# Attention's input, results and statistics in chunks of 384 columns, a loop bound over all tables, and new timetables

## The chip, the cores and the metric

The kernel runs on one core of a Trainium2 chip. The metric is device time in microseconds, the median of several runs. Before the change it is 9664.73 us (three runs, 9664.22 to 9666.31).

## What is computed

Eight images of 256 channels and 48 x 48 = 2304 positions pass two layers, each with a residual: x + layer(groupnorm(x)). Layer 0 is attention over the 16 nearest positions, layer 1 two Mamba blocks (a selective scan) along the positions.

```python
# layer 0
feat_pos = tokens @ W.T + bias            # feat: 256 columns, pos: 256 columns
pos = pos / jnp.maximum(norm, 1e-12)
sim = jnp.einsum('bnc,bmc->bnm', pos, pos)
topksim, topkid = jax.lax.top_k(sim, K)   # K = 16
attn = jax.nn.softmax(topksim, axis=-1)
out = jnp.einsum('bnk,bnkc->bnc', attn, topkfeat)
# layer 1, twice: layernorm, in_proj, convolution of 4 taps, silu, x_proj, softplus, then over t
h = h * jnp.exp(dt_t[:, :, None] * A) + dt_t[:, :, None] * B_t[:, None, :] * x_t[:, :, None]
y = jnp.einsum('bds,bs->bd', h, C_t)      # 512 channels, 16 states each
# then y = (y + xc * D) * silu(z), and out_proj
...
x = x + _L0_conv_ref(_gn(x), ...)
x = x + _L1_conv_ref(_gn(x), ...)
```

## The kernel before

**Units, steps and parts.** The scan is cut in units: one image, one chunk of T = 384 positions (NCH = 6 chunks an image), one of two depths d, so 12 units an image and 96 in all. Their order in an image is (c,d) = 00, 10, 20, 01, 30, 11, 40, 21, 50, 31, 41, 51. A unit has 16 steps of 32 channels (their 16 states lie on the partitions and in four column blocks), and a step has two parts, so a unit has 32 parts and an image 384. The main loop (L1069) runs over parts m, and one part is one scan of two state blocks on DVE (`run_scan`, L886).

**What a part does.** In program order: `carry` and `decay` on ACT (L902, L871: exp of dt times A for the next part, into one of two PSUM buffers), at even parts `make_bx` on POOL (L847: B times dt x, two steps ahead, into one of eight buffers) and `pool_part` on POOL (L914), then the entries of the table `inner` for this m, then the scan, then the entries of `outer`, then one step of the attention of the next image (`ahead.go`). The product of the state with C is made either by POOL for the parts of a step that are marked G in SHARE, or by DVE (L888) right behind the scan for the parts marked V. SHARE has three strings of 32 letters: for units beside attention (order 1 to 9 in the image), for the units around it (0, 10, 11), and for the last image, which has no attention beside it.

**The tables.** All other work of a unit is placed by hand at parts relative to the unit's first one, from -42 (`load_v`) to 40 (`leave` 1): `between` holds what is issued before that part's scan, `behind` what is issued after it. Entries whose place in m falls beside attention use these; all others use `between_spare` and `behind_spare` (L1026, `beside_none`). Every entry issues to the engines' in-order queues: `in_proj`, `step_size`, `x_proj`, `sum_states`, `out_proj` to PE, `load_*` to SP's DMA queue, `tap`, `copy_z`, `silu_*`, `softplus`, `square`, `root` to ACT, `taps`, `center`, `scale`, `gate` to DVE, `times_x` to POOL with two stores on SP. `sum_states` (L926, k = 0 to 3) adds the states of four steps on PE; when it has read them their `bx` buffers come free. `gate` (L937) multiplies the sum by silu(z) on DVE. `out_proj` (L945) makes two halves, and `leave` (L955) takes each out of PSUM: on ACT with a store for d = 0 (`vo`, L963), on DVE for d = 1 (L967). PE's results of the units and of attention share one ring of four PSUM banks (`mm`, L606), so a new result waits until the one four before it is read.

**Attention.** `layer0` is a generator; `ahead.go` takes one step of it per part, the first at m = EARLY. It projects six chunks, waits for a fixed place modulo 16 parts, and then runs 18 blocks of 128 rows, one every 16 parts, by the table `within` (part, function, argument): `similar` (PE, L445), `keep_similar` (ACT, L454), `top` (DVE, L466 to L473, four passes over 2304 columns), `others` (ACT), `turn` (PE), `weights` (ACT), `weigh` (PE), `average` (ACT and the load of x, L520 to L527), `turn_back` (PE), `finish` (L537). `average` of a block loads 128 columns of x (128 KB), and `finish` two parts later adds the block's result to it (DVE, L541), takes `bn_stats` of both channel halves (L543) and stores 128 columns of x1. After the 18 blocks `group_stats` aggregates (L189). Chunk loads of x for layer 0 and the residual of layer 1 share three buffers with the tag "x". Image 0 has its attention before the scan loop, with nothing beside it (`alone`).

Of the kernel before, what the change touches and what calls it, by code (L numbers as in the profile page):

```python
# [8 lines left out]
F32 = mybir.dt.float32  # L9
# [6 lines left out]
P = 128  # L16
# [9 lines left out]
def tile_conv_preact(  # L26
# [18 lines left out]
    nc = tc.nc  # L45
# [5 lines left out]
    CB = C // P  # L51
    DB = DI // P
    NB = N // P
    T = 384
    NCH = N // T
    TB = T // P
# [11 lines left out]
    BLOCK = 16  # L68
    TOPK = (1, 10)
    PHASE = 6  # L70
    EARLY = -24


    SHARE = (
        "GGVGGGVVGGGGGGVGGGVVGGGVGGGGGVVG",
        "GVGGVGVVGVVVGVGVGGGGVGVVGVGVGVGV",
        "VGVGVGVGVGVVGGGVGGGVVGVVGVVGGGVG",
    )
    assert N % T == 0 and N % P == 0 and T % P == 0 and NS % (J * HQ) == 0

# [179 lines left out]
    def layer0(b, left, pool, ps0, alone):  # L260
# [3 lines left out]
        more = 2 if alone else 1  # L264
# [149 lines left out]
        yield  # L414

        x1 = hbm.tile([C, N], F32, tag="x1", name=f"x1_{b}")
        st1 = small.tile([P, CB, NB, 6], F32, tag="gn_st1", name=f"st1_{b}", bufs=1)
        widths = [(c0, min(SW, N - c0)) for c0 in range(0, N, SW)]
        PT = 4
        blocks = [{} for _ in range(NB)]  # L420
# [99 lines left out]
        def average(t):  # L520
            row = blocks[t]
            row["o"] = pool.tile([P, C], F32, tag="o", name=f"o_{b}_{t}", bufs=more)
            nc.scalar.activation(row["o"], row["po"], AF.Identity, scale=row["den"])
            row["xr"] = pool.tile([P, CB, P], F32, tag="xr", name=f"xr_{b}_{t}", bufs=more)
            nc.sync.dma_start(
                row["xr"], x[b, :, t * P : (t + 1) * P].rearrange("(k p) t -> p k t", p=P)
            )  # L527

        def turn_back(t):
            row = blocks[t]  # L530
# [5 lines left out]

        def finish(t):  # L537
            row = blocks[t]
            xr = row["xr"]

            nc.vector.tensor_add(xr, xr, row["pr"].rearrange("p (k t) -> p k t", k=CB))  # L541
            for cb in range(CB):
                nc.vector.bn_stats(st1[:, cb, t, :], xr[:, cb, :])  # L543
            nc.sync.dma_start(x1[:, t * P : (t + 1) * P].rearrange("(k p) t -> p k t", p=P), xr)
            row.clear()


        within = [
            (21, weights, 3), (4, top, 3), (14, turn, 0), (15, weights, 0), (7, others, 3), (-5, similar, 4),
            (-8, keep_similar, 0), (-5, keep_similar, 2), (24, turn_back), (18, weigh, 1), (17, weigh, 0),  # L550
            (1, top, 1), (-9, similar, 0), (-8, similar, 1), (-7, similar, 2), (22, average), (-6, similar, 3),
            (-7, keep_similar, 1), (-3, keep_similar, 3), (0, top, 0), (-3, keep_similar, 4), (15, turn, 1),
            (10, others, 4), (5, others, 0), (3, top, 2), (6, add_top), (11, invert), (5, others, 2),
            (17, turn, 2), (20, turn, 3), (15, weights, 1), (18, turn, 4), (18, weights, 2), (21, weigh, 3),
            (7, others, 1), (19, weigh, 2), (20, weights, 4), (21, weigh, 4), (24, finish),
        ]
        begin = min(part for part, *_ in within)
        parts = {}
# [17 lines left out]
    with tc.tile_pool(name="first", bufs=1) as pool0, tc.tile_pool(  # L576
        name="first_ps", bufs=1, space=PSUM
# [229 lines left out]
    def silu_z(unit):  # L807
# [3 lines left out]
        for e in range(DB - 1):  # L811
# [11 lines left out]
             dt=[], dt_d={}, dtx_d={}, dtr={}, dtxr={}, bx={}, y={}, inw={}, dmat={}, taps={}, xi={}, cv={},  # L823
# [131 lines left out]
    def leave(unit, cb):  # L955
# [16 lines left out]


    between = [
        (-35, center), (7, in_proj, 5), (24, sum_states, 2), (-33, variance), (-21, in_proj, 0),
        (-15, taps, 1), (37, out_proj, 0), (-15, taps, 2), (-14, taps, 3), (-34, square), (39, leave, 0),
        (23, load_rep, "dt", 14), (5, load_rep, "dt", 5), (-4, load_bc, 1), (38, out_proj, 1), (17, load_d, 2),
        (-17, tap, 1), (18, load_rep, "dtx", 13), (-8, times_x, 1), (19, gate, 1), (-22, normal),
        (1, load_rep, "dt", 3), (0, load_rep, "dtx", 4), (15, load_rep, "dt", 10), (6, load_rep, "dtx", 7),
        (10, load_rep, "dtx", 9), (11, gate, 0), (-29, spread_root), (0, times_x, 3), (-19, load_in, 5),  # L980
        (33, load_out), (8, load_rep, "dtx", 8), (-22, load_in, 0), (21, load_rep, "dt", 13), (-20, tap, 0),
        (-10, step_size, 1), (9, copy_z, 2), (-18, in_proj, 2), (2, load_rep, "dtx", 5), (10, sum_states, 0),
        (13, load_rep, "dt", 9), (29, gate, 2), (9, silu_z), (7, load_rep, "dt", 6), (19, load_rep, "dt", 12),
        (-6, load_rep, "dtx", 1), (-14, load_in, 7), (-30, root), (9, load_rep, "dt", 7), (4, load_d, 1),
        (-24, load_in, 3), (17, load_rep, "dt", 11), (14, load_rep, "dtx", 11), (-13, x_proj),
        (-17, load_in, 6), (-3, load_d, 0), (4, load_rep, "dtx", 6), (-4, load_rep, "dtx", 2), (-42, load_v),
    ]
    behind = [
        (-12, split), (-3, load_rep, "dt", 1), (3, in_proj, 4), (-10, step_size, 0), (-3, load_rep, "dt", 0),
        (-8, load_rep, "dtx", 0), (-15, tap, 3), (-1, load_rep, "dt", 2), (-28, scale),  # L990
        (16, load_rep, "dtx", 12), (11, load_rep, "dt", 8), (8, in_proj, 6), (17, sum_states, 1),
        (-14, silu_x), (28, load_rep, "dt", 15), (-39, affine), (2, times_x, 2), (7, copy_z, 0),
        (19, load_rep, "dtx", 14), (10, load_rep, "dtx", 10), (-17, tap, 2), (-10, softplus),
        (-16, in_proj, 3), (3, load_rep, "dt", 4), (-29, load_in, 2), (6, in_proj, 7), (35, gate, 3),
        (-2, load_rep, "dtx", 3), (8, copy_z, 1), (40, leave, 1), (22, load_rep, "dtx", 15), (-8, load_in, 4),
        (29, load_d, 3), (-37, mean), (-19, taps, 0), (-19, in_proj, 1), (-10, load_bc, 0),
        (33, sum_states, 3), (-30, root_end), (-9, times_x, 0), (-20, load_in, 1),
    ]
    between_spare = [
        (24, sum_states, 2), (-34, variance), (-21, in_proj, 0), (38, out_proj, 0), (-15, taps, 2),  # L1000
        (-14, taps, 3), (-35, square), (39, leave, 0), (20, load_rep, "dt", 14), (5, load_rep, "dt", 5),
        (-4, load_bc, 1), (38, out_proj, 1), (17, load_d, 2), (-17, tap, 1), (18, load_rep, "dtx", 13),
        (-8, times_x, 1), (19, gate, 1), (-22, normal), (9, load_rep, "dtx", 8), (1, load_rep, "dt", 3),
        (0, load_rep, "dtx", 4), (14, load_rep, "dt", 10), (6, load_rep, "dtx", 7), (10, load_rep, "dtx", 9),
        (-18, taps, 0), (12, load_rep, "dtx", 10), (17, load_rep, "dtx", 14), (11, gate, 0), (-1, times_x, 2),
        (-19, load_in, 5), (33, load_out), (-22, load_in, 0), (21, load_rep, "dt", 13), (-20, tap, 0),
        (-10, step_size, 1), (9, copy_z, 2), (-18, in_proj, 2), (2, load_rep, "dtx", 5), (10, sum_states, 0),
        (13, load_rep, "dt", 9), (29, gate, 2), (9, silu_z), (7, load_rep, "dt", 6), (19, load_rep, "dt", 12),
        (-6, load_rep, "dtx", 1), (-14, load_in, 7), (37, gate, 3), (-31, root), (9, load_rep, "dt", 7),
        (5, load_d, 1), (-24, load_in, 3), (17, load_rep, "dt", 11), (14, load_rep, "dtx", 11), (-13, x_proj),  # L1010
        (-17, load_in, 6), (-3, load_d, 0), (4, load_rep, "dtx", 6), (-4, load_rep, "dtx", 2), (-42, load_v),
        (-36, center), (-26, spread_root),
    ]
    behind_spare = [
        (-12, split), (-3, load_rep, "dt", 1), (4, in_proj, 4), (-10, step_size, 0), (-5, load_rep, "dt", 0),
        (-8, times_x, 3), (-8, load_rep, "dtx", 0), (-15, tap, 3), (-1, load_rep, "dt", 2),
        (16, load_rep, "dtx", 12), (11, load_rep, "dt", 8), (8, in_proj, 6), (17, sum_states, 1),
        (-14, silu_x), (25, load_rep, "dt", 15), (-39, affine), (6, copy_z, 0), (-17, tap, 2), (-10, softplus),
        (-16, in_proj, 3), (7, in_proj, 5), (3, load_rep, "dt", 4), (-27, load_in, 2), (6, in_proj, 7),
        (-15, taps, 1), (-2, load_rep, "dtx", 3), (8, copy_z, 1), (40, leave, 1), (22, load_rep, "dtx", 15),  # L1020
        (-16, load_in, 4), (29, load_d, 3), (-38, mean), (-21, in_proj, 1), (-12, load_bc, 0),
        (33, sum_states, 3), (-31, root_end), (-9, times_x, 0), (-25, load_in, 1), (-25, scale),
    ]
    place = {(f, *args): part for part, f, *args in between + behind}

# [12 lines left out]
    class Ahead:  # L1038
# [16 lines left out]
        def go(self, m):  # L1055
            if self.image == B or m < EARLY:
                return
# [6 lines left out]
            self.started = self.begun is not None and (m + 1 - PHASE - self.begun) % BLOCK == 0  # L1064

    ahead = Ahead()
    first = min(part for part, *_ in between + behind)
    last = max(part for part, *_ in between + behind)
    for m in range(first, PARTS * NSTEP - HOOKS + last + 1):  # L1069
        n, p = divmod(m, PARTS)  # L1070
        carry(m - 1)
# [56 lines left out]
```

## Time and profile before

| what | value |
|---|---|
| median of three runs | 9664.73 us |
| the profiled execution | 9663.76 us, its span 9661.6 us |
| DVE busy | 8951.2 us |
| POOL busy | 8894.5 us |
| PE / ACT busy | 7986.9 / 7303.4 us |
| L847, `make_bx` on POOL, 1536 times | 5302.0 us, 3458 ns each |
| L871, decays on ACT, 6144 times | 3591.6 us, 585 ns each |
| L886, scans on DVE, 3072 times | 5327.3 us, 1746 and 1753 ns |
| L914, POOL's product, whole steps / half steps | 666 of 3188 ns / 657 of 1692 ns |
| L888, DVE's product of one part, 1083 times | 1037.6 us, 958 ns each |
| first scan | 462.6 us |

Busy time is the union of an engine's instructions. A line of the waits says which instruction of an engine stood idle before it began, and whose end released it: total, times, longest. A line of the timeline has start, duration, engine, source line, operation and tiles, and in brackets the idle time before it.

### The profile page before, as it was taken

The numbers are of one execution on the slowest core, as the hardware profiler recorded it, in microseconds if no ns is written. First come the engines' busy times: TensorE is split into PE (matmuls) and PEld (weight loads), VectorE is DVE, ScalarE is ACT, GpSimd is POOL, SyncE is SP. The second block draws the span as 40 slices with busy tenths as digits, with TensorE's granted clock in tenths as the row PEclk, the third lists the DMA queues.
The fourth block names the chain that finished last, engine by engine and source line by source line (L and its number), as shares of the span: only waits on it lengthen the run. The fifth ranks groups of instructions, "written<-read, shape, count | busy, mean of one in ns | idle before, by whom it ended". The sixth has DMA issues, their size and how long they took to land. (4 is left out here: it accounts for less than half of the span.)

```text
span 9661.6 us, 120523 instructions
## 1 busy us (share of the span) xinstructions
PE 7986.9 (83%) x36761; PEld 4482.3 (46%) x36761; DVE 8951.2 (93%) x7812; ACT 7303.4 (76%) x16018; POOL 8894.5 (92%) x3983
## 2 busy tenths in 40 slices
PE   8888887888878887888878888788887888866665
PEld 6645544455444554445544555444544455432222
DVE  5599998999989999999999999999999999999998
ACT  4587877777777777777777787777787778777776
POOL 1199999999999999999999999999999999999999
PEclk9989998899979998899988999889998899977777
DMA  1134444434444444444444444444444443444443
GB/s 35 57 126 133 125 142 146 135 126 133 136 152 128 132 131 150 136 131 131 135 146 138 130 128 137 146 138 127 135 128 159 128 133 125 143 138 137 148 146 119
DMA packets 1084999, 1267.54 MB, mean 131 GB/s; under 512 B 109728, under 2 KB 1057440, under 8 KB 1084352
## 3 DMA queue, kind: packets, MB, share of 16 engines
q1 hardware_dynamic: 1083808, 1259.83, 40.8%
q8 instruction: 294, 4.82, 0.2%
q14 instruction: 353, 2.89, 0.1%
q10 hardware_dynamic: 544, 0.00, 0.0%
HBM read 1046.58 MB, written 212.86 MB: 130 GB/s over the span
## 5 line engine op out<-in xcount | busy, mean ns | idle before, releaser
L847 POOL TENSOR_TENSOR bx<-BC,dtxr 128x1536 f32<-128x1536 f32 x1536 | 5302.0, 3458 | 124.5 <-PE y L932 106.4
L871 ACT ACTIVATE da<-dtr,A_sb 128x385 f32<-128x385 f32 x6144 | 3591.6, 585 | 960.0 <-DVE bx L886 703.8
L886 DVE TENSOR_TENSOR_SCAN bx<-da,bx 128x770 f32<-128x770 f32 x1989 | 3428.3, 1746 | 153.7 <-ACT da L871 116.9
L914 POOL TENSOR_TENSOR bx<-bx,BC 128x1536 f32<-128x1536 f32 (+1 forms) x1323 | 3234.8, 2445 | 107.6 <-DVE bx L886 101.1
L886 DVE TENSOR_TENSOR_SCAN da<-da,bx 128x770 f32<-128x770 f32 x1083 | 1899.0, 1753 | 65.0 <-ACT da L871 42.3
L932 PE MATMUL y<-bx,sel 128*32 128x384 f32 x12288 | 1323.5, 539 | 181.4 <-POOL bx L914 160.9
L516 PE MATMUL po<-feat,aT 128*128 128x256 f32 x5184 | 1377.7, 415 | 58.1 <-ACT dt L784 44.1
L645 PE MATMUL pe<-vn,inw 128*128 128x384 f32 (+1 forms) x3072 | 1206.0, 524 | 243.8 <-ACT vn L722 71.7
L445 PE MATMUL psim<-pos 128*128 128x512 f32 x2520 | 1220.6, 620 | 100.0 <-DVE xc L745 78.8
L516 PEld LDWEIGHTS po<-feat,aT 128*128 128x128 f32 x5184 | 1036.8, 207 | 405.3 <-ACT dt L784 114.1
L888 DVE TENSOR_TENSOR bx<-da,BC 128x768 f32<-128x768 f32 x1083 | 1037.6, 958 | 37.3
L932 PEld LDWEIGHTS y<-bx,sel 128*32 128x32 f32 x12288 | 426.0, 118 | 1048.7 <-issue 700.9
L645 PEld LDWEIGHTS pe<-vn,inw 128*128 128x128 f32 x3072 | 577.1, 200 | 707.6 <-issue 117.0
L445 PEld LDWEIGHTS psim<-pos 128*128 128x128 f32 x2520 | 501.7, 212 | 649.3 <-issue 382.0
L745 DVE SCALAR_TENSOR_TENSOR xc<-pe,cw,xc 128x384 f32<-128x384 f32 x1152 | 696.0, 611 | 35.0 <-ACT xc L737 8.0
L505 ACT ACTIVATE aT<-pt 128x512 f32<-128x512 f32 (+1 forms) x720 | 387.3, 548 | 354.7 <-PE pt L497 353.1
L496 PE MATMUL pt<-ident,sim 128*128 128x128 f32 x2592 | 551.5, 291 | 104.0 <-ACT sim L454 57.3
L692 PE MATMUL lv<-ones_mean,lsq 128*128 128x1 f32 x1152 | 233.4, 330 | 477.1 <-ACT lsq L686 477.1
L902 ACT COPY h_st<-da 128x2 f32<-128x2 f32 x878 | 139.8, 159 | 583.9 <-DVE bx L888 581.4
L950 PE MATMUL pw<-z,ow 128*128 128x384 f32 x1536 | 539.4, 498 | 42.3 <-DVE z L938 42.0
L775 PE MATMUL pd<-dbl,dtp_sb 16*128 16x384 f32 x768 | 418.4, 691 | 148.2 <-ACT dbl L768 121.5
L496 PEld LDWEIGHTS pt<-ident,sim 128*128 128x128 f32 x2592 | 379.3, 146 | 277.9 <-ACT sim L454 71.6
(156 smaller groups left out, 10322.3 us busy)
## 6 DMA issues: line engine op xcount, KB each, us to landing
dtxr<-dtx_d SPq DMA_DIRECT2D x1536, 192.0 KB, 2.9
dtr<-dt_d SPq DMA_DIRECT2D x1536, 192.0 KB, 2.8
BC<-bc_d SPq DMA_DIRECT2D x192, 768.0 KB, 5.7
inw<-in_in_wT_dram SPq DMA_DIRECT2D x768, 128.0 KB, 2.5
dtx_d<-dtx SPq DMA_DIRECT2D x384, 192.0 KB, 1.9
dt_d<-dt SPq DMA_DIRECT2D x384, 192.0 KB, 2.1
ow<-in_out_wT_dram SPq DMA_DIRECT2D x96, 512.0 KB, 4.1
dmat<-diag SPq DMA_DIRECT2D x384, 64.0 KB, 3.2
```

Source lines behind the costliest of these rows:

```text
L445: nc.tensor.matmul(pm, pos[:, k, t * P : (t + 1) * P], pos[:, k, c0 : c0 + w], start=(k == 0), stop=(k == CB - 1),)
L496: nc.tensor.transpose(pt[:, q], row["sim"][:, r], ident)
L516: nc.tensor.matmul(row["po"], aT[:, m % PT, :], feat[:, m, :], start=(m == 0), stop=(m == NB - 1))
L645: nc.tensor.matmul(pe, w[:, k], unit["vn"][:, k, lo:], start=(k == 0), stop=(k == CB - 1))
L745: nc.vector.scalar_tensor_tensor(unit["xc"][e], unit["pe"][e][:, k : k + T], cw[:, unit["d"], e, k : k + 1], unit["xc"][e], ALU.mult, ALU.add,
L847: nc.gpsimd.tensor_tensor(bx[:, :, 1:], unit["BC"][0], unit["dtxr"][i].unsqueeze(1).to_broadcast([P, Q, T]), ALU.mult,)
L871: nc.scalar.activation(da[:, s * (1 + T) : (s + 1) * (1 + T)], unit["dtr"][i], AF.Exp, scale=A_sb[:, unit["d"], i, p * HQ + s : p * HQ + s ...
L886: nc.vector.tensor_tensor_scan(h, da, g, 0.0, ALU.mult, ALU.add)
L888: nc.vector.tensor_tensor(bx[:, :, 0:T], da.rearrange("p (q t) -> p q t", q=HQ)[:, :, 1:], unit["BC"][1][:, qs], ALU.mult,)
L914: nc.gpsimd.tensor_tensor(g[:, :, 0:T], g[:, :, 1:], unit["BC"][1][:, qs], ALU.mult)
L932: nc.tensor.matmul(y[j * G : (j + 1) * G, :], sel, unit["bx"][k * J + j][:, q, 0:T], start=False, stop=True, skip_group_check=True,)
L950: nc.tensor.matmul(pw, unit["ow"][:, k, cb * P : (cb + 1) * P], unit["z"][k], start=(k == 0), stop=(k == DB - 1),)
```

## The change

Four edits, in code:

```diff
-    EARLY = -24
+    EARLY = -22
...
-        "GGVGGGVVGGGGGGVGGGVVGGGVGGGGGVVG",
-        "GVGGVGVVGVVVGVGVGGGGVGVVGVGVGVGV",
-        "VGVGVGVGVGVVGGGVGGGVVGVVGVVGGGVG",
+        "GGVGGGVGGGVVGGVGGGGVGGGVGGGGGVVG",
+        "GVGGGGVVGGVVGGGVVGGGVGVVGVGVGVGV",
+        "VVVGVVGGVGVVGGGVGGGVGGVVGVVGGGVG",
...
-        st1 = small.tile([P, CB, NB, 6], F32, tag="gn_st1", name=f"st1_{b}", bufs=1)
+        rows = {}
+        st1 = small.tile([P, CB, NCH, 6], F32, tag="gn_st1", name=f"st1_{b}", bufs=1)
...
             nc.scalar.activation(row["o"], row["po"], AF.Identity, scale=row["den"])
-            row["xr"] = pool.tile([P, CB, P], F32, tag="xr", name=f"xr_{b}_{t}", bufs=more)
-            nc.sync.dma_start(
-                row["xr"], x[b, :, t * P : (t + 1) * P].rearrange("(k p) t -> p k t", p=P)
-            )
+            if t % TB == 0:
+                tag, bufs = ("xr", 2) if alone else ("x", 3)
+                rows[t // TB] = load_chunk(pool, x[b], t // TB, tag, f"xr_{b}_{t}", bufs)
...
-            xr = row["xr"]
-
+            c, j = divmod(t, TB)
+            xr = rows[c][:, :, j * P : (j + 1) * P]
             nc.vector.tensor_add(xr, xr, row["pr"].rearrange("p (k t) -> p k t", k=CB))
-            for cb in range(CB):
-                nc.vector.bn_stats(st1[:, cb, t, :], xr[:, cb, :])
-            nc.sync.dma_start(x1[:, t * P : (t + 1) * P].rearrange("(k p) t -> p k t", p=P), xr)
+            if j + 1 == TB:
+                xr = rows.pop(c)
+                for cb in range(CB):
+                    nc.vector.bn_stats(st1[:, cb, c, :], xr[:, cb, :])
+                nc.sync.dma_start(x1[:, c * T : (c + 1) * T].rearrange("(k p) t -> p k t", p=P), xr)
...
-    first = min(part for part, *_ in between + behind)
-    last = max(part for part, *_ in between + behind)
+    every = between + behind + between_spare + behind_spare
+    first = min(part for part, *_ in every)
+    last = max(part for part, *_ in every)
```

The rows of x, of the sum and of its statistics are thus kept by chunks of three blocks: one load of 384 KB at the first block's `average`, one store and two `bn_stats` of 384 columns at the third block's `finish`. The loop's bounds are taken over the spare tables too. In the tables these entries change their part (b: `between`, before the scan; h: `behind`, after it); all others keep theirs:

| table | entry: from -> to |
|---|---|
| within | top 0: 0 -> -1; invert: 11 -> 12; weigh 0: 17 -> 16; weigh 2: 19 -> 20; weights 4: 20 -> 19 |
| between, behind | square: -34 b -> -35 h; load_in 1: -20 h -> -21 b; load_rep dt 0: -3 h -> -3 b; times_x 3: 0 b -> -3 b; load_d 1: 4 b -> 5 h; in_proj 7: 6 h -> 5 h; copy_z 1: 8 h -> 8 b; gate 1: 19 b -> 21 b; sum_states 2: 24 b -> 25 b; gate 2: 29 b -> 29 h; sum_states 3: 33 h -> 32 b; leave 1: 40 h -> 38 h |
| spare tables | center: -36 b -> -37 h; spread_root: -26 b -> -29 b; scale: -25 h -> -28 h; taps 3: -14 b -> -14 h; load_rep dt 0: -5 h -> -5 b; load_rep dt 2: -1 h -> -1 b; load_rep dtx 9: 10 b -> 11 b; load_rep dt 14: 20 b -> 23 b; sum_states 2: 24 b -> 25 b; gate 2: 29 b -> 31 b; load_d 3: 29 h -> 29 b |

More of the change, by code (lines that the diff above doesn't have):

```diff
@@ L538, in finish @@
             row = blocks[t]
-            xr = row["xr"]
+            c, j = divmod(t, TB)
+            xr = rows[c][:, :, j * P : (j + 1) * P]
             nc.vector.tensor_add(xr, xr, row["pr"].rearrange("p (k t) -> p k t", k=CB))
-            for cb in range(CB):
-                nc.vector.bn_stats(st1[:, cb, t, :], xr[:, cb, :])
-            nc.sync.dma_start(x1[:, t * P : (t + 1) * P].rearrange("(k p) t -> p k t", p=P), xr)
+            if j + 1 == TB:
[3 more added lines that the diff above has]
+                nc.sync.dma_start(x1[:, c * T : (c + 1) * T].rearrange("(k p) t -> p k t", p=P), xr)
             row.clear()
         within = [
[L549 to L555, printed above, removed]
+            (21, weights, 3), (20, weigh, 2), (4, top, 3), (14, turn, 0), (15, weights, 0), (7, others, 3),
+            (-5, similar, 4), (-8, keep_similar, 0), (-5, keep_similar, 2), (24, turn_back), (18, weigh, 1),
+            (16, weigh, 0), (1, top, 1), (-9, similar, 0), (-8, similar, 1), (-7, similar, 2), (22, average),
+            (-6, similar, 3), (-7, keep_similar, 1), (-3, keep_similar, 3), (-1, top, 0),
+            (-3, keep_similar, 4), (15, turn, 1), (10, others, 4), (5, others, 0), (3, top, 2), (6, add_top),
+            (12, invert), (5, others, 2), (17, turn, 2), (20, turn, 3), (24, finish), (15, weights, 1),
+            (18, turn, 4), (18, weights, 2), (21, weigh, 3), (7, others, 1), (19, weights, 4), (21, weigh, 4),
         ]
@@ L974, in tile_conv_preact @@
     between = [
-        (-35, center), (7, in_proj, 5), (24, sum_states, 2), (-33, variance), (-21, in_proj, 0),
-        (-15, taps, 1), (37, out_proj, 0), (-15, taps, 2), (-14, taps, 3), (-34, square), (39, leave, 0),
+        (-35, center), (7, in_proj, 5), (25, sum_states, 2), (-33, variance), (-21, in_proj, 0),
+        (-15, taps, 1), (37, out_proj, 0), (-15, taps, 2), (-14, taps, 3), (32, sum_states, 3), (39, leave, 0),
         (23, load_rep, "dt", 14), (5, load_rep, "dt", 5), (-4, load_bc, 1), (38, out_proj, 1), (17, load_d, 2),
-        (-17, tap, 1), (18, load_rep, "dtx", 13), (-8, times_x, 1), (19, gate, 1), (-22, normal),
+        (-17, tap, 1), (18, load_rep, "dtx", 13), (-8, times_x, 1), (21, gate, 1), (-22, normal),
@@ L979, in tile_conv_preact @@
         (1, load_rep, "dt", 3), (0, load_rep, "dtx", 4), (15, load_rep, "dt", 10), (6, load_rep, "dtx", 7),
[L980 to L983, printed above, removed]
@@ L984, in tile_conv_preact @@
-        (-6, load_rep, "dtx", 1), (-14, load_in, 7), (-30, root), (9, load_rep, "dt", 7), (4, load_d, 1),
+        (10, load_rep, "dtx", 9), (11, gate, 0), (-29, spread_root), (-20, tap, 0), (-3, times_x, 3),
+        (-19, load_in, 5), (33, load_out), (-3, load_rep, "dt", 0), (8, load_rep, "dtx", 8), (-22, load_in, 0),
+        (21, load_rep, "dt", 13), (-10, step_size, 1), (9, copy_z, 2), (-18, in_proj, 2),
+        (2, load_rep, "dtx", 5), (-21, load_in, 1), (10, sum_states, 0), (13, load_rep, "dt", 9), (9, silu_z),
@@ new lines, in tile_conv_preact @@
+        (7, load_rep, "dt", 6), (19, load_rep, "dt", 12), (-6, load_rep, "dtx", 1), (-14, load_in, 7),
+        (-30, root), (9, load_rep, "dt", 7), (-24, load_in, 3), (17, load_rep, "dt", 11),
+        (14, load_rep, "dtx", 11), (-13, x_proj), (8, copy_z, 1), (-17, load_in, 6), (-3, load_d, 0),
+        (4, load_rep, "dtx", 6), (-4, load_rep, "dtx", 2), (-42, load_v),
+    ]
+    behind = [
+        (-12, split), (3, in_proj, 4), (-10, step_size, 0), (-8, load_rep, "dtx", 0), (-15, tap, 3),
+        (-1, load_rep, "dt", 2), (-28, scale), (16, load_rep, "dtx", 12), (-35, square),
+        (11, load_rep, "dt", 8), (8, in_proj, 6), (17, sum_states, 1), (-14, silu_x), (28, load_rep, "dt", 15),
+        (-39, affine), (2, times_x, 2), (7, copy_z, 0), (19, load_rep, "dtx", 14), (10, load_rep, "dtx", 10),
+        (-17, tap, 2), (-10, softplus), (-16, in_proj, 3), (35, gate, 3), (3, load_rep, "dt", 4),
+        (-3, load_rep, "dt", 1), (-29, load_in, 2), (5, in_proj, 7), (-2, load_rep, "dtx", 3), (38, leave, 1),
+        (22, load_rep, "dtx", 15), (-8, load_in, 4), (29, load_d, 3), (-37, mean), (-19, taps, 0),
+        (5, load_d, 1), (-19, in_proj, 1), (-10, load_bc, 0), (-30, root_end), (-9, times_x, 0), (29, gate, 2),
+    ]
@@ new lines, in tile_conv_preact @@
+    between_spare = [
+        (25, sum_states, 2), (-34, variance), (-21, in_proj, 0), (38, out_proj, 0), (-15, taps, 2),
+        (-35, square), (39, leave, 0), (23, load_rep, "dt", 14), (5, load_rep, "dt", 5),
+        (-1, load_rep, "dt", 2), (-4, load_bc, 1), (38, out_proj, 1), (17, load_d, 2), (-17, tap, 1),
+        (18, load_rep, "dtx", 13), (-8, times_x, 1), (19, gate, 1), (-22, normal), (9, load_rep, "dtx", 8),
+        (1, load_rep, "dt", 3), (0, load_rep, "dtx", 4), (14, load_rep, "dt", 10), (6, load_rep, "dtx", 7),
+        (11, load_rep, "dtx", 9), (-18, taps, 0), (12, load_rep, "dtx", 10), (17, load_rep, "dtx", 14),
+        (11, gate, 0), (-1, times_x, 2), (-19, load_in, 5), (33, load_out), (-22, load_in, 0), (29, load_d, 3),
+        (21, load_rep, "dt", 13), (-20, tap, 0), (-10, step_size, 1), (-5, load_rep, "dt", 0), (9, copy_z, 2),
+        (-18, in_proj, 2), (2, load_rep, "dtx", 5), (10, sum_states, 0), (13, load_rep, "dt", 9),
+        (31, gate, 2), (9, silu_z), (7, load_rep, "dt", 6), (19, load_rep, "dt", 12), (-6, load_rep, "dtx", 1),
+        (-14, load_in, 7), (37, gate, 3), (-31, root), (9, load_rep, "dt", 7), (5, load_d, 1),
@@ L985, in tile_conv_preact @@
         (-24, load_in, 3), (17, load_rep, "dt", 11), (14, load_rep, "dtx", 11), (-13, x_proj),
         (-17, load_in, 6), (-3, load_d, 0), (4, load_rep, "dtx", 6), (-4, load_rep, "dtx", 2), (-42, load_v),
[L987 to L1012, printed above, removed]
@@ L1013, in tile_conv_preact @@
+        (-29, spread_root),
     ]
     behind_spare = [
-        (-12, split), (-3, load_rep, "dt", 1), (4, in_proj, 4), (-10, step_size, 0), (-5, load_rep, "dt", 0),
-        (-8, times_x, 3), (-8, load_rep, "dtx", 0), (-15, tap, 3), (-1, load_rep, "dt", 2),
+        (40, leave, 1), (-12, split), (-14, taps, 3), (-3, load_rep, "dt", 1), (4, in_proj, 4),
+        (-10, step_size, 0), (-8, times_x, 3), (-8, load_rep, "dtx", 0), (-15, tap, 3),
         (16, load_rep, "dtx", 12), (11, load_rep, "dt", 8), (8, in_proj, 6), (17, sum_states, 1),
@@ L1019, in tile_conv_preact @@
         (-16, in_proj, 3), (7, in_proj, 5), (3, load_rep, "dt", 4), (-27, load_in, 2), (6, in_proj, 7),
-        (-15, taps, 1), (-2, load_rep, "dtx", 3), (8, copy_z, 1), (40, leave, 1), (22, load_rep, "dtx", 15),
-        (-16, load_in, 4), (29, load_d, 3), (-38, mean), (-21, in_proj, 1), (-12, load_bc, 0),
-        (33, sum_states, 3), (-31, root_end), (-9, times_x, 0), (-25, load_in, 1), (-25, scale),
+        (-15, taps, 1), (-2, load_rep, "dtx", 3), (8, copy_z, 1), (22, load_rep, "dtx", 15), (-16, load_in, 4),
+        (-38, mean), (-37, center), (-21, in_proj, 1), (-12, load_bc, 0), (33, sum_states, 3), (-31, root_end),
+        (-9, times_x, 0), (-25, load_in, 1), (-28, scale),
     ]
```

## The prediction

> **What bounds the kernel now.** I read the page's first part, then the busy times by stage, the groups by shape, the waits of DVE and POOL inside one stage, and last the timeline around the longest waits. The page:
>
> ```profile
> span 9661.6 us, 120523 instructions
> PE 7986.9 (83%) x36761; PEld 4482.3 (46%) x36761; DVE 8951.2 (93%) x7812; ACT 7303.4 (76%) x16018; POOL 8894.5 (92%) x3983
> ```
>
> DVE and POOL are level. The loop begins at 462.6 us. The stages of image 2's period (one unit beside chunk work, nine beside attention, two beside its end), and the last image with nothing beside it; columns: length, then the busy time of PE, PEld, DVE, ACT, POOL.
>
> ```profile
> 2797.00:2890.80 93.80, 72.78 (x328) 39.76 (x328) 84.81 (x76) 71.67 (x155) 87.80 (x62) 0.83 0.43 138
> 2890.80:3771.60 880.80, 772.35 (x3611) 439.85 (x3609) 853.31 (x732) 692.30 (x1527) 855.43 (x326) 0.91 0.41 131
> 3771.60:3964.40 192.80, 144.64 (x658) 78.74 (x658) 172.72 (x165) 144.58 (x315) 175.62 (x104) 0.83 0.49 157
> 8618.50:9648.00 1029.50, 666.94 (x2604) 276.55 (x2606) 943.71 (x800) 734.19 (x1615) 1019.01 (x435) 0.76 0.43 139
> ```
>
> Beside attention (63 units of 97.9 us) DVE idles 27.5/9 = 3.1 us a unit, POOL 25.4/9 = 2.8. In the 21 units around it both idle some 6 to 10 us. In the last 12 units POOL idles 10.5 us in all: it is the bound. So a gain has to come from waits that stop DVE and POOL together, or from work taken off both. The waits in the nine units (totals, times, longest):
>
> ```profile
> DVE z L938 <- PE y L932: 7.5, 7, 2.4
> DVE bx L886 <- ACT da L871: 7.5, 9, 1.3
> POOL bx L847 <- PE y L932: 10.5, 5, 4.7
> POOL bx L914 <- DVE bx L886: 6.9, 10, 1.1
> ```
>
> `gate` (L938) waits for `sum_states` on PE, and POOL's `make_bx` (L847) waits for the same sums, which free its buffers. The longest case, in the image's fifth unit, on PE, DVE and POOL:
>
> ```profile
> 3210.44 1.82 PE L645 MATMUL pe<-vn,inw 128*128 128x384 f32 x4 [1.88 <-DVE xr L967]
> ...
> 3218.11 2.79 PE L932 MATMUL y<-bx,sel 128*32 128x384 f32 x32
> ```
> ```profile
> 3209.80 0.59 DVE L967 SCALAR_TENSOR_TENSOR xr<-pw,b_feat,xr 128x384 f32<-128x384 f32 x1
> ...
> 3221.12 0.56 DVE L938 TENSOR_TENSOR z<-y,z 128x384 f32<-128x384 f32 x1 [2.44 <-PE y L932]
> ```
> ```profile
> 3220.96 3.46 POOL L847 TENSOR_TENSOR bx<-BC,dtxr 128x1536 f32<-128x1536 f32 x1 [4.75 <-PE y L932]
> ```
>
> `leave` 1 at part 40 is what gives a PSUM bank back (3209.80). PE's next projection waits 1.88 us for it, all behind it in PE's queue slides, the sum ends late, and DVE stands 2.44 us, POOL 4.75 us. The seventh unit shows the same (2.4 and 3.6 us).
>
> **The change part by part.**
>
> *Chunks of 384.* Per image 36 `bn_stats` become 12, 18 loads and 18 stores 6 and 6; the 18 additions stay. The rows:
>
> ```profile
> L543 DVE BATCH_NORM_STATS2 st<-xr 128x6 f32<-128x128 f32 x288 | 70.1, 285 | 5.0
> L247 DVE BATCH_NORM_STATS2 st<-xs 128x6 f32<-128x384 f32 x96 | 48.4, 546 | 31.8 <-DMA xs<-in_x_dram 31.5
> ```
>
> They overlap at their ends, so I count busy time: 70.1/8 = 8.8 us an image (243 ns each) against 48.4/8 = 6.1 (504 ns): 2.7 us of DVE. The aggregation reads 6 groups in place of 18 (282 ns for 608, twice): 0.65. [...] The two rows give (504 - 243)/256 = 1.02 ns an element and a fixed part of 243 - 131 = 112 ns, so 2.7[...]. Beside scans that is 7 x 3.4 = 24 us of DVE [...]; as POOL is level with DVE, between 0 and 24 reaches the end. I take half, 12. Image 0's share lies where PE is busy 95% (windows from 100 to 300 us): nothing.
>
> The 384 KB load of x is now wanted two parts after its issue, as the 128 KB one was. A load of that size lands in 4.8 us (xs), the small one in 3.1; the additions came at least 10.5 us after the issue in the old trace. Covered: 0. Uncovered it would cost 1 to 2 us six times an image. SP issues for some 31 us of a 97 us unit; 24 issues fewer per image, and 12 waits for `finish` in its queue, are between 0 and a small gain: 0.
>
> *Last part of all tables.* `last` was 40 and stays 40, now from the spare table: nothing. EARLY moves image 1's first chunks by two parts in the first unit, and attention starts on the next multiple of 16 all the same: 0, within 1 us.
>
> *SHARE.* One POOL multiplication of half a step takes 1692 ns, a whole step 3188; DVE's own takes 958. Beside attention: from 5 halves and 9 wholes to 7 and 8, +0.20 us of POOL a unit, DVE the same. Around it: from 10 and 3 to 8 and 5, +2.99 of POOL, -1.92 of DVE. Last image: from 11 and 3 to 7 and 5, -0.39.
>
> *leave 1 from 40 to 38* (places 32 to 319; elsewhere it stays at 40). The bank comes back two parts sooner, and the 1.88 us before the projection go. What is late next: gate 0's scan needs the decay that ACT ended by 3218.3, before the gate could start. So 1.9 of the 2.44 us go, in two units of nine: 2 x 1.9 x 7 = 27 us (bounds 0 and 34).
>
> It adds a wait: `out_proj` 1 is queued at the same part 38, so DVE (every second unit) or ACT stands until it ends, with scans, or decays and state copies, behind it. In the old trace it ended at 3202.15, and DVE came from its scan and multiplication at 3200.04: 2.1 us. But `top` 0 (2.55 us) moves from part 0 to -1, ahead of that scan, so DVE comes at about 3202.5. I count 0; without that cover 2.1 us.
>
> *sum_states 3 from 33 behind the scan to 32 before it.* The fifth unit again, on PE, DVE and ACT:
>
> ```profile
> 3186.77 2.35 PE L445 MATMUL psim<-pos 128*128 128x512 f32 x4
> 3188.96 0.81 PE L929 MATMUL y<-xc,dmat 128*128 128x384 f32 x2
> 3189.70 2.79 PE L932 MATMUL y<-bx,sel 128*32 128x384 f32 x32
> ```
> ```profile
> 3192.64 0.56 DVE L938 TENSOR_TENSOR z<-y,z 128x384 f32<-128x384 f32 x1 [1.11 <-PE y L932]
> ```
> ```profile
> 3193.59 0.37 ACT L454 COPY sim<-psim 128x256 f32<-128x256 f32 x1 [1.96 <-PE psim L445]
> 3193.86 1.21 ACT L871 ACTIVATE da<-dtr,A_sb 128x385 f32<-128x385 f32 x2
> ```
>
> The sum goes ahead of one similarity block (2.35 us) and ends before DVE wants it; POOL's product was there at 3186.2. That wait is 0.5 to 1.1 us in six of the nine units, 0.56 us a unit over all 63 (35 us). But the last similarity block ends no sooner, and ACT's copy of it holds the decay for a later scan. So part comes back as a wait for `da`: I take 20 of 35 (bounds 0 and 35).
>
> *Other moves.* `gate` 1 and 2 and `sum_states` 2 later, `times_x` 3 earlier with its two stores and POOL's 1 us, in_proj 7 earlier, the LayerNorm chain of the spare tables earlier. All issue the same instructions, on engines whose waits there are zero or belong to ACT's long blocks (4.4 us before one scan in the unit before the chunk work). No row shows a gain; loss and gain are bounded by those waits, about 1 us a unit either way. I take 0.
>
> *Sum.* Beside attention: -27 - 20 - 12 + 63 x 0.20 (12, as POOL is level) = -47. Around it: POOL alone would make 21 x 2.99 = +63, DVE alone 21 x -1.92 = -40. In 20 units each idles 6 to 10 us, so neither decides; a decay's bank comes free 0.96 us sooner where DVE no longer multiplies, and I take -0.65 a unit, -13. The unit after the last attention has a full POOL: +3. Together -10. Last image: 12 x -0.39 = -5. In all -62 us. The profiled execution ran 9663.8 us (its span and 2.2 around), 0.9 below the median; 9601.8, and as a median 9603 us.
>
> **Rivals.**
>
> *More is set free.* The first unit beside attention runs in 96.1 us with 1.0 us of POOL idle. If all 63 came to that (1.8 x 63 = 113, less 12), and the units around lost 2 us each (40): 9665 - 146 = 9519. For it: most waits start in the one chain above. Against: the unit with c = 0, d = 1 (99.9 us) waits for a POOL memset that no move touches.
>
> *The waits only move.* Four PSUM banks are shared by attention and the units; another allocation becomes the late one, and only 12 + 5 stay against 12: about 9660. For it: PE also waits for ACT's copies and for `vn`. Against: both waits named have a direct cause, which is taken away.
>
> *Slower: leave 1 stands for out_proj 1.* At part 38 (part 6 of the next unit). Price 2.1 us, 63 times: 132, less the 62: 9735. It decides once DVE or ACT stands over 1.0 us there (62/63), thus once `out_proj` 1 ends 1 us later, against the scans, than in the old trace. Against: the cover by `top` 0, and a sum that leaves PE sooner.
>
> **How the numbers follow.** About 0.2% is what a measurement of this kernel tells from no change: 9645 to 9684. Likeliest case, 9570 to 9640: 0.45. More set free, 9500 to 9570: 0.20. Waits only move, 9640 to 9684: 0.19, of which 0.08 still below 9645. Slower by the wait, 9684 to 9750: 0.14. Beyond 9500: 0.02. Faster 0.75, same 0.11, slower 0.14. The range 9515 to 9675 leaves out some 0.05 below and 0.15 above.
>
> **What would show it.** Right: the 70.1 us of L543 become about 48; PE's wait for DVE xr L967 and POOL's for PE y L932 much smaller; gate's wait below half of 125.2 us; mean unit beside attention near 97.1 us; ACT's wait for psim larger. Wrong: new idle time before L967 or before `vo` at part 6 (the slower rival); a DMA as releaser of L541 (the load isn't covered); POOL full in the units around attention with those units longer (the price of SHARE).

## The result, and the profile after

The changed kernel runs in 9640.5 us (median of 13 runs, 9633.9 to 9647.9) against 9662.9 for the kernel before beside it: ratio 0.9976, 95% interval 0.9968 to 0.9984. It is 22 us faster, a third of the 62 that were forecast, and inside the forecast range. The first lines of its page:

```profile
span 9645.9 us, 120209 instructions
PE 7904.1 (82%) x36761; PEld 4385.8 (45%) x36761; DVE 8923.6 (93%) x7578; ACT 7294.2 (76%) x16026; POOL 8959.1 (93%) x4022
```

The same stages of image 2's period and of the last image, columns as before:

```profile
2797.00:2892.30 95.30, 69.41 (x318) 36.59 (x319) 82.63 (x73) 70.14 (x150) 90.07 (x63) 0.88 0.43 139
2892.30:3763.40 871.10, 760.00 (x3616) 427.45 (x3618) 849.40 (x709) 692.21 (x1535) 855.67 (x334) 0.93 0.40 132
3763.40:3960.80 197.40, 141.64 (x655) 77.11 (x654) 175.30 (x161) 144.08 (x313) 182.02 (x105) 0.83 0.47 155
8612.30:9633.30 1021.00, 676.89 (x2607) 280.61 (x2608) 942.31 (x800) 730.68 (x1595) 1014.21 (x410) 0.77 0.43 140
```

The nine units beside attention went from 880.8 to 871.1 us (96.8 a unit, forecast 97.1), and the last image's 12 units lost 8.5 us. What was gained there is lost around attention: 93.8 to 95.3 us, and 192.8 to 197.4. Over the whole run the 63 units beside attention gain 63.6 us, the 12 of the last image 8.6, the 21 around attention lose 54.4, and the first scan comes 3 us later. (Unit lengths, here and below, run from first scan to first scan in the one profiled execution of each kernel; the one of the kernel after is the slowest of its 13, 7.4 us above the median.) The forecast had -47, -5, -10 and 0: only the units around attention are far on the wrong side.

**Where it went.** The units behind the end of attention (order 10 in the image, counted from 0) grew most, from a mean of 98.4 to 103.0 us. DVE's idle time in them is the old one (9.5 and 9.7 us), so it is DVE's own time that grew. The group that stands out is the addition of `b_feat` to the group means in `group_stats`, two elements a partition, before:

```profile
L191 DVE TENSOR_TENSOR mv_b<-mv_b,b_feat 128x2 f32<-128x2 f32 x8 | 8.4, 1044 | 0.3
```

and after:

```profile
L191 DVE TENSOR_TENSOR mv_b<-mv_b,b_feat 128x2 f32<-128x2 f32 x8 | 50.0, 6253 | 0.3
```

The change does not touch this line. Of the eight, image 0's takes 0.16 us, with POOL idle; each of the other seven takes 7.05 to 7.16 us, where it took 1.16 to 1.19. That is 41.6 us more, about the 40 us by which the forecast missed, though other terms missed too, in both directions. The timeline of the kernel after, DVE and then POOL:

```profile
3807.36 0.48 DVE L189 BATCH_NORM_AGGREGATE mv_b<-st 128x2 f32<-128x36 f32 x2
3807.88 7.05 DVE L191 TENSOR_TENSOR mv_b<-mv_b,b_feat 128x2 f32<-128x2 f32 x1
3814.85 1.75 DVE L888 TENSOR_TENSOR_SCAN da<-da,bx 128x770 f32<-128x770 f32 x1
```
```profile
3806.40 3.48 POOL L849 TENSOR_TENSOR bx<-BC,dtxr 128x1536 f32<-128x1536 f32 x1
3809.78 1.73 POOL L916 TENSOR_TENSOR bx<-bx,BC 128x768 f32<-128x768 f32 x1
3811.42 3.50 POOL L849 TENSOR_TENSOR bx<-BC,dtxr 128x1536 f32<-128x1536 f32 x1
3821.24 1.69 POOL L916 TENSOR_TENSOR bx<-bx,BC 128x768 f32<-128x768 f32 x1 [6.33 <-DVE bx L888]
```

The addition ends at 3814.93, when POOL's third operation ends (3814.92) and POOL itself has to wait for a scan. Such a record counts as busy time, so DVE's own waits do not name it (0.3 us of idle time before the group, as before the change); what shows is PE's wait for its result, 43.8 us before and 85.9 after:

```profile
PE pm_b L194 <- DVE mv_b L191: 85.9, 8, 12.0
```

In the kernel before, the addition met one POOL operation and ended with it, at 3819.86 and 3819.84:

```profile
3818.70 1.16 DVE L191 TENSOR_TENSOR mv_b<-mv_b,b_feat 128x2 f32<-128x2 f32 x1
```
```profile
3816.41 3.43 POOL L847 TENSOR_TENSOR bx<-BC,dtxr 128x1536 f32<-128x1536 f32 x1
```

The big DVE operations of the loop have one input in PSUM (the decays, `pw`, `pr`), and this addition has both in SBUF. My theory, not shown by these two traces: because of that the addition stands until POOL pauses (in the seven images after the first it ends 0.01 to 0.02 us after POOL's operation in both kernels), and SHARE, which gives POOL more work around attention, took the pause away. Rivals: POOL's 3 us more a unit (SHARE as such), and the new spare tables.

### The profile page after: what moved, and what is told of

Its sections match the earlier page's. It is cut to its first block, busy times and chain, and to the rows that moved or that the text cites. A ratio compares the mean times of both kernels' runs of the same rounds, so it can differ in the third digit from the quotient of the medians.

```text
span 9645.9 us, 120209 instructions
## 1 busy us (share of the span) xinstructions
PE 7904.1 (82%) x36761; PEld 4385.8 (45%) x36761; DVE 8923.6 (93%) x7578; ACT 7294.2 (76%) x16026; POOL 8959.1 (93%) x4022
## 5 line engine op out<-in xcount | busy, mean ns | idle before, releaser
L849 POOL TENSOR_TENSOR bx<-BC,dtxr 128x1536 f32<-128x1536 f32 x1536 | 5301.5, 3456 | 33.2 <-PE y L934 27.5
L888 DVE TENSOR_TENSOR_SCAN bx<-da,bx 128x770 f32<-128x770 f32 x2031 | 3507.3, 1747 | 204.0 <-ACT da L873 165.7
L916 POOL TENSOR_TENSOR bx<-bx,BC 128x768 f32<-128x768 f32 (+1 forms) x1362 | 3300.7, 2423 | 170.0 <-DVE bx L888 168.3
L888 DVE TENSOR_TENSOR_SCAN da<-da,bx 128x770 f32<-128x770 f32 x1041 | 1824.8, 1753 | 63.8 <-ACT da L873 45.9
L446 PE MATMUL psim<-pos 128*128 128x512 f32 x2520 | 1198.2, 610 | 178.7 <-DVE xr L541 79.0
L890 DVE TENSOR_TENSOR bx<-da,BC 128x768 f32<-128x768 f32 x1041 | 997.6, 958 | 35.8
L446 PEld LDWEIGHTS psim<-pos 128*128 128x128 f32 x2520 | 480.6, 203 | 692.9 <-issue 352.2
L931 PE MATMUL y<-xc,dmat 128*128 128x384 f32 x768 | 416.5, 631 | 128.5 <-ACT dt L786 32.8
L489 ACT ACTIVATE rest<-left,three 128x512 bf16<-128x512 f32 (+1 forms) x720 | 453.3, 668 | 68.5 <-DVE left L474 68.5
L498 PE MATMUL pt<-minus,rest 128*128 128x128 bf16 x2592 | 493.1, 225 | 7.4 <-ACT rest L489 7.4
```

The source lines that it names most:

```text
L446: nc.tensor.matmul(pm, pos[:, k, t * P : (t + 1) * P], pos[:, k, c0 : c0 + w], start=(k == 0), stop=(k == CB - 1),)
L849: nc.gpsimd.tensor_tensor(bx[:, :, 1:], unit["BC"][0], unit["dtxr"][i].unsqueeze(1).to_broadcast([P, Q, T]), ALU.mult,)
L888: nc.vector.tensor_tensor_scan(h, da, g, 0.0, ALU.mult, ALU.add)
L890: nc.vector.tensor_tensor(bx[:, :, 0:T], da.rearrange("p (q t) -> p q t", q=HQ)[:, :, 1:], unit["BC"][1][:, qs], ALU.mult,)
L916: nc.gpsimd.tensor_tensor(g[:, :, 0:T], g[:, :, 1:], unit["BC"][1][:, qs], ALU.mult)
```

## The experiments

Times are medians, ratios are to the kernel before on the same chip.

**1. The addition without a second SBUF tensor** (`a1_bias_tensor_scalar`), in the kernel after:

```diff
-            nc.vector.tensor_add(mv[:, :, 0], mv[:, :, 0], more)
+            for cb in range(CB):
+                nc.vector.tensor_scalar(mv[:, cb, 0:1], mv[:, cb, 0:1], more[:, cb : cb + 1], None, ALU.add)
```

> The kernel after the change, with the addition of b_feat to the group means (two elements a partition, L191) as two tensor_scalar instructions with a per-partition scalar instead of one tensor_add of two SBUF tensors. Theory [...]: the add stands 7.1 us in each of seven image periods because it has two SBUF inputs and POOL's queue runs without a gap; then these instructions take some 0.1 to 0.2 us each, and the time falls by 7 x 5 to 6 us, from 9640 to about 9600. Rival (SHARE): DVE only waits there for a POOL that bounds those units anyway; then the long instruction goes, DVE waits at the next scan or product instead, and the time stays within 10 us of 9640. If tensor_scalar is held as well, it shows some 7 us in the first of the two.

Measured 9592.8 us, ratio 0.9928 (0.9915 to 0.9940): 48 us below the kernel after. The group, and DVE's timeline at the same place, while POOL runs its operations from 3786.69 to 3798.40 without a gap:

```profile
L192 DVE TENSOR_SCALAR mv_b<-mv_b,b_feat 128x1 f32<-128x1 f32 x16 | 2.7, 186 | 0.0
```
```profile
3791.08 0.34 DVE L192 TENSOR_SCALAR mv_b<-mv_b,b_feat 128x1 f32<-128x1 f32 x2
3791.33 1.76 DVE L889 TENSOR_TENSOR_SCAN da<-da,bx 128x770 f32<-128x770 f32 x1
```

The same sum at the same place in DVE's order, with one tensor and a scalar a partition, takes 186 ns in the mean of 16, and the run is 48 us shorter: the wait was on the path, and POOL did not bound these units. That two tensors, or a small size, do not bring the wait by themselves shows in the kernel after. L541 is the same operation with `pr` in PSUM, and takes 0.40 to 0.42 us in all 144 records, 115 of them inside a POOL operation. L182 takes two tensors of three elements a partition, one of them (`lv`) in PSUM; of its 96 records 94 lie inside a POOL operation, each 0.16 us long:

```profile
L182 DVE SCALAR_TENSOR_TENSOR rs<-lv,rs 128x3 f32<-128x3 f32 x96 | 15.4, 160 | 3.3
```

**2. SHARE, tables and both.** In the kernel after, the SHARE string of the units around attention as before (`a2_share1_old`), the spare tables as before (`a3_spare_old`), and the string with the other addition (`a4_bias_share1_old`). The string (the old table entries are in the table under "The change"):

```diff
-        "GVGGGGVVGGVVGGGVVGGGVGVVGVGVGVGV",
+        "GVGGVGVVGVVVGVGVGGGGVGVVGVGVGVGV",
```

> The kernel after the change, with only the SHARE string of the units around attention as before the change (16 V instead of 14). Theory [...]: POOL's queue has its old gap again behind the make_bx that the add meets, the add takes about 1.2 us, and 7 x 6 = 42 us go, to some 9598; the rest of those units changes by less than 1 us each. Rival (SHARE as such): POOL has 3.0 us less in each of 21 units, and they fall by more than the add's time, 9580 or less. Rival (tables): the time stays within 15 us of 9640, with the units beside the chunk work still 1.5 us longer than before the change.

> The kernel after the change, with the two spare tables (units around attention, and the last image) as before the change. Theory [...]: the add still takes 7 us, and the time stays between 9625 and 9650. Rival (tables): the units around attention lose the time that they gained in length (about 54 us over 21 units), and the time falls to some 9590 to 9610.

> The kernel after the change, with both the tensor_scalar form of the b_feat addition and the old SHARE string for the units around attention. Theory [...]: with the add short already by the old string, the other form brings only its last 1 us an image: within 10 us below a2_share1_old, some 9590. Against a1_bias_tensor_scalar it shows what the SHARE string alone is worth once the add is out of the way: the theory says less than 15 us either way.

| kernel | us | ratio | the addition, images 1 to 7 |
|---|---|---|---|
| after | 9640.5 | 0.9976 | 7.05 to 7.16 us |
| a2_share1_old | 9590.5 | 0.9925 (0.9913 to 0.9937) | 1.15 to 1.55 |
| a3_spare_old | 9627.6 | 0.9963 (0.9950 to 0.9975) | 7.27 to 7.29 |
| a1_bias_tensor_scalar | 9592.8 | 0.9928 (0.9915 to 0.9940) | 0.15 to 0.22, twice |
| a4_bias_share1_old | 9587.6 | 0.9924 (0.9912 to 0.9936) | 0.15 to 0.21, twice |

The old string alone brings 50 us and the short addition back; once the addition is out of the way the string is worth 5 us (a4 against a1), less than these runs can tell apart. So the rival "SHARE as such" falls: POOL's 3 us a unit cost little, the lost pause cost the rest. The new spare tables cost 13 us (the intervals just touch), and not by this wait, which stays long without them.

**3. SHARE alone, in the kernel before** (`b6_share1_new`): only that string new.

> The kernel before the change, with only the new SHARE string for the units around attention. Theory ([...] set off by SHARE): POOL comes to the add two operations later, its queue holds no gap, and the add takes about 7 us in each of seven image periods: 7 x 6 = 42 us more, 9690 to 9715. Rival: the long add needs the chunks too (the add comes 0.65 us sooner with them); then it stays at 1.2 us and the time between 9650 and 9680.

Measured 9688.7 us, ratio 1.0026 (1.0016 to 1.0035): 26 us slower. The group, and POOL's timeline around an addition that runs from 3820.47 to 3826.35:

```profile
L191 DVE TENSOR_TENSOR mv_b<-mv_b,b_feat 128x2 f32<-128x2 f32 x8 | 41.2, 5146 | 0.3
```
```profile
3817.84 3.49 POOL L847 TENSOR_TENSOR bx<-BC,dtxr 128x1536 f32<-128x1536 f32 x1
3821.25 1.72 POOL L914 TENSOR_TENSOR bx<-bx,BC 128x768 f32<-128x768 f32 x1
3822.88 3.46 POOL L847 TENSOR_TENSOR bx<-BC,dtxr 128x1536 f32<-128x1536 f32 x1
```

The string alone makes the addition long: 7 x 4.7 = 33 us, where the whole run is 26 us longer and its units around attention 28.8, so a few us came back elsewhere. I expected 42 us more and 7 us an addition: here it comes later within POOL's run of three operations, and stands 5.9. The chunks are not needed, and alone (`b1_chunks`, below) they leave it at 1.3 us; with them the addition came a little sooner within the run.

**4. The prediction's other steps, one by one, in the kernel before.** The chunks alone (`b1_chunks`: only the edits of `average`, `finish` and `st1`):

> The kernel before the change, with only x, results and statistics in chunks of 384 columns; tables, SHARE and EARLY as before. The prediction's step: 12 us less (bounds 0 and 24), so about 9651, with the load of x never the releaser of the addition. Theory [...]: the add keeps about 1.2 to 2 us, since POOL's queue there is the old one. If the chunks are what makes the add long, it takes 7 us here, and the time is 20 to 40 us over 9663.

Measured 9622.1 us, ratio 0.9957 (0.9943 to 0.9971): 41 us less, three times the 12. The window of the nine units beside attention, to be read against the 880.8, 853.31 (DVE) and 855.43 (POOL) of before (its first 0.5 us lie ahead of them):

```profile
2879.90:3754.90 875.00, 767.94 (x3609) 434.45 (x3608) 850.87 (x709) 691.48 (x1527) 855.15 (x326) 0.92 0.41 132
```

To part DVE's time from the queue's, chunks only for the transfers (`b7_chunk_dma`) and only for the statistics (`b8_chunk_stats`); the added lines, shown in part:

```diff
# b7: bn_stats per block of 128 again, into st1 of NB groups
+            for cb in range(CB):
+                nc.vector.bn_stats(st1[:, cb, t, :], xr[:, cb, :])
# b8: load into, and store from, a slice of the chunk's buffer per block
+            nc.sync.dma_start(x1[:, t * P : (t + 1) * P].rearrange("(k p) t -> p k t", p=P), xr)
```

> The kernel before the change, with x loaded and x1 stored in chunks of 384 columns, and bn_stats still per block of 128 columns. It asks where the 41 us of the chunks come from. Theory (DVE time): nothing changes on DVE, so within 8 us of 9663. Rival (SP's queue): 24 issues and 12 waits less per image let the other loads land sooner, and 15 us or more go.

> The kernel before the change, with x loaded and x1 stored per block of 128 columns into a chunk's buffer, and bn_stats once per chunk of 384 columns. Theory (DVE time): all of the 41 us of the chunks come here, 9620 to 9635. Rival (SP's queue): no more than the DVE time saved, 24 us, so 9639 or more.

b7 9663.2 us, ratio 1.0001 (0.9992 to 1.0009); b8 9625.9, ratio 0.9960 (0.9948 to 0.9973). The statistics bring all that can be told from noise, the transfers nothing.

`leave` 1 at 38, with `top` 0 at -1 (`b2_leave38_top`) and without (`b3_leave38`), and `sum_states` 3 at 32 (`b4_sum32`); b2 and b3 also take the loop's bounds over all tables, since part 40 is then in the spare tables alone:

```diff
-(40, leave, 1)           # b2 and b3, in behind
+(38, leave, 1)
-(0, top, 0)              # b2 alone, in within
+(-1, top, 0)
-(33, sum_states, 3)      # b4, from behind to between
+(32, sum_states, 3)
```

> The kernel before the change, with leave 1 at part 38 instead of 40 in the tables beside attention, top 0 at part -1 instead of 0, and the loop's bounds over all tables. The prediction's step: PE no longer waits 1.9 us for DVE xr L967 in the fifth and seventh unit, 27 us less (bounds 0 and 34), so about 9636, and no idle time before leave 1. Slower rival: DVE or ACT stands 2 us for out_proj 1 in most units, 9700 or more.

> As b2_leave38_top, but top 0 stays at part 0, so that its 2.55 us no longer lie ahead of leave 1. The prediction's step: without that cover DVE (or ACT) stands about 2.1 us for out_proj 1 in up to 63 units; DVE idle time before xr L967 of some 50 us or more, and the time above b2_leave38_top by 30 us or more. If the cover is not needed, it is within 10 us of b2_leave38_top.

> The kernel before the change, with only sum_states 3 at part 32 ahead of the scan instead of part 33 behind it, beside attention. The prediction's step: gate 3's wait at part 3 goes (35 us in all), 15 of it come back as DVE's wait for the decay, since ACT stands longer at the last similarity copy; 20 us less (bounds 0 and 35), about 9643. If no wait comes back: 9628. If PE's order makes another result late: 9663 or more.

| kernel | us | ratio | against before | forecast |
|---|---|---|---|---|
| b2_leave38_top | 9635.8 | 0.9973 (0.9962 to 0.9984) | -26 | -27 |
| b3_leave38 | 9686.7 | 1.0026 (1.0016 to 1.0036) | +25, 51 above b2 | 30 or more above b2 |
| b4_sum32 | 9641.5 | 0.9979 (0.9972 to 0.9986) | -21 | -20 |

PE's wait for the PSUM bank (30.1 us before), in b2:

```profile
PE pe L645 <- DVE xr L967: 3.7, 5, 1.0
```

DVE's wait for `out_proj` 1 in b3, where the cover is missing (4.4 us before):

```profile
DVE xr L967 <- PE pw L950: 48.5, 30, 2.2
```

and in b4, where the gate's 125.2 us fall and the decay's 116.9 rise:

```profile
DVE bx L886 <- ACT da L871: 130.4, 103, 4.4
DVE z L938 <- PE y L932: 92.5, 40, 6.6
```

**5. What the runs point to** (`a5_bias_share1_spare_old`): the kernel after with the other addition, the old string and the old spare tables.

> The kernel after the change with the tensor_scalar form of the b_feat addition, the old SHARE string for the units around attention, and the old spare tables. With the spare tables alone put back, the kernel after the change ran 13 us faster; if that adds to the 53 us of the other two, this is about 9575 and the fastest of all. Rival: the 13 us were of the same wait, and it stays at 9588 within 5 us.

9584.6 us, ratio 0.9918 (0.9904 to 0.9931), the fastest measured, 78 us below the kernel before. Against a4 it is 3 us, less than these runs can tell: of the spare tables' 13 us nothing is left in the time once the addition is short. The units around attention are shorter with the old ones in both pairs (2045.1 to 2028.2 us in a3, 2000.7 to 1984.3 in a5), but these sums differ by up to 14 us among b-runs that share tables and string there, so what the new spare tables cost stays open.

## Why the prediction was right and wrong

- **Chunks of 384** (-12, bounds 0 to 24): measured -41, outside the bounds. The saved DVE time was right: busy 8951.2 us before and 8926.2 in b1, 20.9 of these 25.0 us in the 63 units. The step "half of it reaches the end, as POOL is level" was wrong, and so was the upper bound: DVE's idle time fell as well, from 27.5 to 24.1 us in nine units. What fell is the gate's wait for the sums (125.2 to 113.6 us, of it 54.6 to 36.2 in the 63 units), and POOL's wait for DVE's scans (101.1 to 77.1); the decay's did not. A likely reading is that the sums wait for POOL's products and these for DVE's scans, so that DVE gets back part of what it gives. That is not shown, nor why the second part is nearly as large as the first. "The load is covered" and "the issues bring nothing": right together, b7 is no change.
- **leave 1 at 38** (-27), **its cover by `top` 0** (2.1 us without it): b2 measured -26. PE's 14 waits of 1.9 us, which the sum counts, are gone, and in b3 DVE stands 2.15 us in the unit that was reckoned. But the size is in part luck: the units that were counted (order 4 and 6) give 1.4 and 1.5 us each in b2, 20 in all, and order 3, which was not, gives 1.9, 13 in all. That gain is absent in b3, so it is tied to `top` 0. And ACT, which takes `out_proj` 1 out of PSUM in six of the nine units, stands 42.4 us before `vo` in b2, against nothing before and 0 in the forecast.
- **The slower rival.** In the whole change the cover is thinner: `sum_states` 3 and the gates come sooner, and DVE reaches `leave` 1 before `out_proj` 1 has ended. It stands 30.0 us in three of the nine units (34.2 over the run), and ACT 80.6 us in the other six:

```profile
ACT vo L965 <- PE pw L952: 80.6, 42, 3.8
```

  That is 110.6/63 = 1.8 us a unit, over the 1.0 from which the rival was to decide, and these units are 63.6 us shorter all the same. So the wait came, and its price was wrong: not every us that ACT stood was one of the kernel's. The decay's wait on DVE, through which ACT's delay reaches it, grew by 19.5 us in these units (54.5 to 74.0). The kernel after, DVE:

```profile
3198.13 0.96 DVE L890 TENSOR_TENSOR bx<-da,BC 128x768 f32<-128x768 f32 x1
3200.76 1.14 DVE L969 SCALAR_TENSOR_TENSOR xr<-pw,b_feat,xr 128x384 f32<-128x384 f32 x2 [1.67 <-PE pw L952]
```

- **sum_states 3 at 32** (-20 of 35): right in size; b4 measured -21, and the gate's wait fell by 36.0 us in the 63 units. Some 15 us came back as forecast, but in these units as a wait of `scale` for PE's `lb` (from none to 14.7), while the decay's wait grew by 3.1 there; the rest of its growth lies outside them.
- **Together beside attention** (-47): -63.6. The three alone sum to -41 - 26 - 21 = -88 over the whole run; some 24 us of that do not appear. DVE's waits in the 63 units show two reasons. The gate's wait for PE, 54.6 us before, is 36.2 in b1, 30.3 in b2 and 18.6 in b4: alone, the moves take 78.7 us off a wait of 54.6, and together they can only take all of it, 24 us less. And the 30.0 us before `leave` 1 come in only where the moves meet. The decay's growth is no more than the sum of the single runs (1.2, 15.1 and 3.1). No run parts the two reasons, nor the new SHARE string beside attention, +12 in the forecast, which was not run alone. The kernel after, waits of DVE over the whole run (the gate's 80.0 lie outside the 63 units):

```profile
DVE bx L888 <- ACT da L873: 165.7, 163, 4.4
DVE z L940 <- PE y L934: 80.0, 32, 5.5
...
DVE xr L969 <- PE pw L952: 34.2, 23, 2.4
```

- **SHARE around attention** (-10): this is the step that failed. Those units are 54.4 us longer, and putting the old string back brings 50 us. Of the 54.4, 41.6 are the addition's; the spare tables' 13 to 17 lie in the same units, and the string's own work gives back 3.5 (a1 against a4), where -10 was forecast. It weighed 2.99 us of POOL against 1.92 of DVE and the idle time of both, and found that neither decides. That held for the work itself (a4 against a1: 5 us). It left out that here the two engines were not independent: one DVE instruction stood until POOL paused (1.16 to 1.19 us an image before), and the new order of POOL's work took the pause away (7.05 to 7.16 us). The sum had no term for it. The row was in the profile of before: 1044 ns for two elements a partition, 0.16 us where POOL was idle. Of the sign that was named for this, POOL full and the units longer, only the second came: POOL idles 145 us in them (158 before).
- **Spare tables, EARLY, loop bounds** (0): the spare tables cost 13 us in the kernel after and nothing that the time shows against a4. EARLY and the bounds were not tried alone; the first scan came 3 us later.
- **Last image** (-5): -8.6.
- **More is set free**, the faster rival: its argument against itself, that the unit with c = 0, d = 1 waits for a POOL memset that no move touches, did not hold. That unit (order 3) gained most, 99.9 to 96.2 us, which is 26 of the 63.6 us; the chunks alone give 1.6 of its 3.7, b2 1.9.
- **The signs.** L543's 70.1 us became 49.0 (about 48 forecast), and PE's wait for DVE xr L967 went. The gate's wait fell to 80.0 us, not below half of 125.2, and ACT's wait for `psim` fell where a rise was forecast (109.3 to 49.9).
- With the addition out of the way the whole change is worth 9662.9 - 9592.8 = 70 us, so the rest of the sum (62) was near in total, by errors of both signs: the chunks too small, the meeting of the moves left out.

## What to carry to other kernels

When work is moved between DVE and POOL, look for DVE rows whose duration does not fit their size. In this kernel the addition of two tensors in SBUF was one: 7.05 to 7.16 us for two elements a partition, 0.16 with POOL idle, a wait in the guise of work that DVE's list of waits did not show. This sum was better done with a scalar operand (a1, 186 ns each). One input in PSUM might have served as well, since L182 took 0.16 us inside a POOL operation; that was not tried on this sum. DVE and POOL were level and waited for each other, and time taken from DVE brought more than itself (25 us brought 41). Gains that shorten the same wait did not add up (78.7 us alone, of a wait of 54.6).

## What the runs showed of the hardware that was not expected

A DVE addition of two elements a partition with both inputs in SBUF did not end between two POOL operations that followed each other at once: it stood through three (5.9 us in b6, 7.1 in the kernel after) and ended within 0.1 us of the moment at which POOL stopped. With one POOL operation left it stood 1.2 us, with POOL idle it took 0.16. With a scalar a partition in place of the second tensor, the two instructions of one image took 0.34 us in the middle of a POOL operation (a1), and all 16 took 186 ns in the mean.
